# Pairwise products of 32 fields: eight-kilobyte packets for GpSimd's loads, and an output ring with three equal slots

## The chip, the cores and the metric

The kernel runs on one core of one Trainium2 chip. The metric is the time of one execution on the device, in microseconds (us), as the median of several runs. One execution was recorded by the hardware profiler; it has a time of its own beside the medians.

## The reference

There are 4096 rows of 32 fields with 64 numbers each, all in float32. For each of the 496 pairs of fields i < j, field i is multiplied with a 64 × 64 matrix of that pair, and the result is multiplied element by element with field j:

```
i_idx, j_idx = np.triu_indices(32, k=1)
vdotw = jnp.einsum('bpd,pde->bpe', inputs[:, i_idx, :], W)   # W: (496, 64, 64)
out = (vdotw * inputs[:, j_idx, :]).reshape(4096, 496 * 64)
```

The output has 4096 × 31,744 numbers, 520 MB. The inputs are 33.5 MB of rows and 8.1 MB of matrices.

## The kernel before, in words

**Tiles.** The rows are worked on in 32 tiles of 128 (NT in the code), one row on each of the 128 partitions. A tile has 31,744 output columns, 496 units of 64 columns. Of a tile's fields, two at a time make a pass: pass p has fields 2p and 2p+1, and its output is field 2p with all later fields, followed by field 2p+1 with all later ones. The loop (L198 to L248) runs over the tiles, in a tile over the passes, and in a pass over chunks of up to 512 columns.

**Compute.** TensorE transposes a tile's fields (L182), in two halves: the second at pass 3 of the tile itself, the first half of the next tile at pass 9. ACT copies them from PSUM to SBUF (L183). For each chunk TensorE multiplies the field 2p and the field 2p+1 with their weights (L222) into two banks of PSUM, taken round the eight banks. VectorE multiplies both with the later fields and writes the output ring in SBUF: one instruction with two rows of columns for a full chunk (L232), single ones for the ends (L240). The two rows that one instruction writes lie a whole field's width apart in the output, up to 31 units.

**The ring and the stores.** The ring (L185) has 28,160 columns, 440 units, for each partition. A tile is cut into four groups of passes (STORES, L17) with 118, 102, 123 and 153 units. Each group takes a place in the ring behind the one before; if it doesn't fit to the end, it begins at the ring's start (L204), and the rest of the ring stays unused that time. Behind a group SP issues one store of it (L246), 128 rows of 26 to 39 KB. VectorE must wait until the store that last read a place of the ring has landed.

**The loads.** There are three slots for tiles of x, filled two tiles at a time (x_slots, L34): tile 0 alone, tiles 1 and 2 at the start, then tiles 3 and 4 when tile 2 begins, and so on. The weights are resident; SP loads them in five pieces (L194) before the loop. Of a pair of tiles the odd one is loaded by ACT (L157), 8 KB for each partition. The even tiles 2 to 26 (LIGHT_TILES) are loaded by GpSimd, in another way (load_beside, L131); pairs without such a tile are loaded by ACT in one transfer, 16 KB for each partition.

**load_beside.** The 16 DMA engines share a transfer. The code holds[...] that engine 4 (LIGHT) should be given less to do. A tile is therefore loaded in two parts: 120 partitions (HEAD) by the fifteen engines other than LIGHT, and the last 8 partitions by two engines, other ones from tile to tile (PAIRS_FROM). [...] The fifteen engines take the 120 rows in two halves each, in packets of 4 KB. The host lays x out in the order in which it is read, with small gaps (PAD).

**Order.** SP's queue has the weights and then the stores in order of their groups. ACT's has its loads and the copies of the transposes, GpSimd's only its loads. Nothing else sets the order; each engine runs its program and waits on semaphores.

Of the kernel before, what the change touches and what calls it, by code (L numbers as in the profile page):

```python
# [9 lines left out]
F32 = mybir.dt.float32  # L10
ALU = mybir.AluOpType

P = 128
BANK = 512
BANKS = 8

STORES = [[0, 1], [2, 3], [4, 5, 6], [7, 8, 9, 10, 11, 12, 13, 14, 15]]  # L17

LOADS = [[0], [1], [2, 3], [4, 5, 6], [7, 8, 9, 10, 11, 12, 13, 14, 15]]


FIRST_HALF_AT, SECOND_HALF_AT = 9, 3
RING = 28160

DMA_ENGINES = 16
LIGHT = 4
LIGHT_TILES = range(2, 28, 2)
PAIRS_FROM = [6, 8, 10, 12, 14, 0, 1]
HEAD = P - P % (DMA_ENGINES - 1)
REST = (P - HEAD) // 2  # L30
PAD = 16


def x_slots(NT):  # L34


    loads = [[(0, 0)]]
    for t in range(1, NT, 2):
        if t + 1 == NT:
            loads.append([(t, 1)])  # L40
        elif loads[-1][-1] == (t - 1, 2):
            loads.append([(t + 1, 0), (t, 1)])
        else:
            loads.append([(t, 1), (t + 1, 2)])
    return loads


@with_exitstack
def pair_bilinear_kernel(
    ctx: ExitStack,  # L50
    tc: tile.TileContext,
    x: bass.AP,
    w: bass.AP,
    out: bass.AP,
    F: int,
    D: int,
):

    nc = tc.nc
    NT = out.shape[1] * 2 // (F * (F - 1) * D)
    NPR = F // 2

    width = [(F - 1 - i) * D for i in range(F)]
    off = [sum(width[:i]) for i in range(F)]
    cols = sum(width)


    woff = [i % 2 * D + sum(width[i % 2 : i : 2]) for i in range(F)]
    store_w = [sum(width[2 * p] + width[2 * p + 1] for p in g) for g in STORES]

    const = ctx.enter_context(tc.tile_pool(name="const", bufs=1))
    psum = ctx.enter_context(tc.tile_pool(name="ps", bufs=1, space=bass.MemoryType.PSUM))

    ident = const.tile([P, P], F32, tag="ident", name="ident")
    make_identity(nc, ident)

    def runs(tl, a, b, n):  # L100

        ap = tl[:, a : a + n]
        return bass.AP(ap.tensor, ap.offset, [list(ap.ap[0]), [b - a, 2], list(ap.ap[1])])

    xbuf = const.tile([P, 3 * F * D], F32, tag="x", name="x")
    x_loads = x_slots(NT)
    x_sizes = [
        sum(P * F * D + (2 * PAD if t in LIGHT_TILES else 0) for t, s in load) for load in x_loads
    ]
    slot = {t: xbuf[:, ts(s, F * D)] for load in x_loads for t, s in load}  # L110

    nudges = [const.tile([DMA_ENGINES, 16], F32, tag=f"nudge{i}", name=f"nudge{i}") for i in range(2)]
    cursor = 0

    def from_pool(out, in_):

        tc.keep_in_program_order(nc.gpsimd.dma_start(out=out, in_=in_))  # L117

    def from_engine(e):

        nonlocal cursor
        k = (e - cursor) % DMA_ENGINES
        if k:
            nudge = nudges[e == LIGHT + 1]
            from_pool(
                nudge[:k].rearrange("p (h c) -> p h c", h=2)[:, :, :4],
                x[: k * 8].rearrange("(p h c) -> p h c", p=k, h=2),
            )
        cursor = e

    def load_beside(at, xt, lap):  # L131

        nonlocal cursor
        n = F * D
        from_engine(PAIRS_FROM[lap % len(PAIRS_FROM)])
        g = REST * n + PAD
        tail = x[at + HEAD * n : at + HEAD * n + 2 * g].rearrange("(g c) -> g c", g=2)
        from_pool(xt[HEAD:], tail[:, : REST * n])
        cursor += 2
        from_engine(LIGHT + 1)  # L140
        from_pool(
            xt[:HEAD].rearrange("p (h c) -> p h c", h=2),
            x[at : at + HEAD * n].rearrange("(h p c) -> p h c", h=2, p=HEAD),
        )
        cursor = LIGHT

    def load_x(load):

        at = sum(x_sizes[: x_loads.index(load)])
        parts = [[(t, s)] for t, s in load] if any(t in LIGHT_TILES for t, s in load) else [load]  # L150
        for part in parts:
            t, s = part[0]
            n = len(part) * F * D
            if t in LIGHT_TILES:
                load_beside(at, slot[t], LIGHT_TILES.index(t))
            else:
                nc.scalar.dma_start(  # L157
                    out=xbuf[:, s * F * D : s * F * D + n],
                    in_=x[at : at + P * n].rearrange("(p c) -> p c", p=P),
                )  # L160
            at += P * n + (2 * PAD if t in LIGHT_TILES else 0)

    pring = psum.tile([P, BANKS * BANK], F32, tag="pring", name="pring")
    bank = 0

    def take_banks(n):

        nonlocal bank
        if bank + n > BANKS:
            bank = 0  # L170
        got = pring[:, bank * BANK : (bank + n) * BANK]
        bank = (bank + n) % BANKS
        return got

    xT = const.tile([P, NPR * P], F32, tag="xT", name="xT")

    def transpose_x(xt, g):

        n = 2 * BANK // P
        pt = take_banks(2)  # L180
        for c in range(n):
            nc.tensor.transpose(pt[:, ts(c, P)], xt[:, ts(n * g + c, P)], ident)  # L182
        nc.scalar.copy(xT[:, ts(g, 2 * BANK)], pt)  # L183

    ring = const.tile([P, RING], F32, tag="ring", name="ring")  # L185
    at = 0

    load_x(x_loads[0])
    w_sb = const.tile([P, sum(width[0::2])], F32, tag="w", name="w")
    done = 0  # L190
    for g in LOADS:

        upto = woff[2 * g[-1]] + width[2 * g[-1]]
        nc.sync.dma_start(out=w_sb[:, done:upto], in_=w[:, done:upto])  # L194
        done = upto

    transpose_x(slot[0], 0)
    for t in range(NT):  # L198
        xt = slot[t]
        for load in x_loads:  # L200
            if min(load)[0] == t + 1:
                load_x(load)
        for s, group in enumerate(STORES):
            if at + store_w[s] > RING:  # L204
                at = 0
            osb = ring[:, at : at + store_w[s]]
            at += store_w[s]
            o0 = off[2 * group[0]]
            for p in group:
                if p == SECOND_HALF_AT:  # L210
                    transpose_x(xt, 1)
                if p == FIRST_HALF_AT and t + 1 < NT:
                    transpose_x(slot[t + 1], 0)
                first = (width[2 * p] - 1) % BANK + 1
                for c1 in range(first, width[2 * p] + 1, BANK):
                    n = first if c1 == first else BANK
                    c0 = c1 - n
                    odd = width[2 * p + 1] and c1 > D
                    pm = take_banks(2)
                    for h in range(1 + bool(odd)):  # L220
                        a = woff[2 * p + h] + c0 - h * D
                        nc.tensor.matmul(  # L222
                            pm[:, h * BANK : h * BANK + n],
                            xT[h * D : (h + 1) * D, ts(p, P)],
                            w_sb[h * D : (h + 1) * D, a : a + n],
                            start=True,
                            stop=True,
                        )
                    xj = xt[:, (2 * p + 1) * D + c0 : (2 * p + 1) * D + c1]
                    o = [off[2 * p + h] - o0 + c0 - h * D for h in range(2)]  # L230
                    if odd and (c0 or c1 < width[2 * p]):
                        nc.vector.tensor_tensor(  # L232
                            runs(osb, o[0], o[1], n),
                            runs(pm, 0, BANK, n),
                            bass.AP(xj.tensor, xj.offset, [xj.ap[0], [0, 2], xj.ap[1]]),
                            ALU.mult,
                        )
                    else:
                        for h in range(1 + bool(odd)):
                            nc.vector.tensor_tensor(  # L240
                                osb[:, o[h] + h * D : o[h] + n],
                                pm[:, h * (BANK + D) : h * BANK + n],
                                xj[:, h * D :],
                                ALU.mult,
                            )
            nc.sync.dma_start(  # L246
                out=out[:, t * cols + o0 : t * cols + o0 + store_w[s]], in_=osb
            )  # L248


# [44 lines left out]
```

## Time and profile before

| | |
|---|---|
| median of 9 runs | 1325.56 us (1325.04 to 1326.89) |
| the profiled execution: its time | 1325.36 us |
| its span on the core | 1323.2 us |
| PE (TensorE) busy | 1165.3 us, 88% |
| DVE (VectorE) busy | 1183.5 us, 89% |
| ACT, POOL (GpSimd) busy | 66.1 us, 32.5 us |
| DMA: bytes, mean rate | 562.90 MB, 425 GB/s |
| the same stores, by group: issue to landing, median | 19.5, 17.6, 18.4 and 17.1 us (118, 102, 123 and 153 units) |
| ACT's loads of one tile, issue to landing | 18.9 us |
| GpSimd's loads of 120 partitions, issue to landing | 33.7 us |

The span is the time from the first to the last event on the core. An engine's busy time is the sum of its instructions' durations, where instructions that overlap count double. The DMA rows of the profile are those of the sixteen DMA engines together; "share" is the time that packets took, over sixteen times the span. A packet here is one contiguous piece that a DMA engine moves: for a store, one partition's row of the group. In the wait list, "A <- B: 75.2, 40, 6.1" means that engine A waited for B 75.2 us in total, 40 times, 6.1 us at the longest.

### The profile page before, as it was taken

What the parts mean: (1) busy time and instruction counts of PE and PEld (TensorE: products, weight loads), DVE (VectorE), ACT (ScalarE), POOL (GpSimd) and SP (SyncE); (2) the same over time, 40 slices, a digit from 0 to 9 for tenths busy, and PEclk for the clock granted to TensorE, in tenths of its full rate; (3) what the DMA queues carried; (4) which work ended last, traced back from release to release, by engine and by line L of the source; (5) the groups of instructions that cost most, each with busy time, mean ns of one, the idle gap of its engine ahead of it and who ended that gap; (6) DMA issues with size and microseconds to landing.
All of it is one profiled execution on the core that took longest, in us unless ns stands there. A gap on an engine that the chain in (4) does not pass through costs nothing.

```text
span 1323.2 us, 13175 instructions
## 1 busy us (share of the span) xinstructions
PE 1165.3 (88%) x5376; PEld 549.1 (41%) x5376; DVE 1183.5 (89%) x1376; ACT 66.1 (5%) x65; POOL 32.5 (2%) x58
## 2 busy tenths in 40 slices
PE   5998989989898998998989989898988989989893
PEld 3443444444343434444334444334444434443441
DVE  4998989989899998998989899898988989989894
ACT  0000000000000000000000000000000000000000
POOL 1000000000000000000000000000000000000000
PEclk9998999989999998998999999999999999999997
DMA  9999999999999999999999999999999999999998
GB/s 334 429 431 431 430 432 431 432 430 423 429 433 427 433 427 429 429 428 433 428 428 429 432 429 427 429 429 433 431 429 429 430 430 431 425 436 432 425 424 357
DMA packets 27068, 562.90 MB, mean 425 GB/s; under 512 B 4584, under 2 KB 4584, under 8 KB 7960
## 3 DMA queue, kind: packets, MB, share of 16 engines
q1 hardware_dynamic: 19152, 528.49, 93.4%
q10 hardware_dynamic: 2448, 19.92, 3.6%
q0 software_dynamic: 5408, 13.65, 2.7%
q8 instruction: 42, 0.69, 0.2%
q14 instruction: 18, 0.15, 0.0%
HBM read 41.95 MB, written 520.09 MB: 425 GB/s over the span
## 4 chain that ended last, share of the span: by engine, by line
DMA 47%; DVE 37%; issue 9%; PE 5%; DVEq 0%; ACT 0%
DMA out_dram<-ring 46%; DVE ring L232 32%; PE pring L222 5%; DVE ring L240 5%; DMA x<-in_x_dram 1%; PE pring L182 0%; DVEq L232 0%; ACT xT L183 0%; DVEq L291 0%; DVEq L240 0%
## 5 line engine op out<-in xcount | busy, mean ns | idle before, releaser
L222 PE MATMUL pring<-w,xT 64*128 64x512 f32 (+4 forms) x4864 | 1100.7, 563 | 128.6 <-DVE ring L232 111.3
L232 DVE TENSOR_TENSOR ring<-pring,x 128x1024 f32<-128x1024 f32 (+3 forms) x1056 | 1104.1, 1105 | 114.5 <-DMA out_dram<-ring 75.2
L222 PEld LDWEIGHTS pring<-w,xT 64*128 64x128 f32 x4864 | 491.8, 191 | 693.5 <-DVE ring L232 521.1
L183 ACT COPY xT<-pring 128x1024 f32<-128x1024 f32 x64 | 64.8, 1012 | 1212.1 <-PE pring L182 1189.7
L240 DVE TENSOR_TENSOR ring<-pring,x 128x64 f32<-128x64 f32 (+3 forms) x320 | 97.2, 352 | 7.4 <-DMA out_dram<-ring 6.5
L182 PEld LDWEIGHTS pring<-ident,x 128*128 128x128 f32 x512 | 57.2, 145 | 60.9 <-DVE ring L232 50.4
L182 PE MATMUL pring<-ident,x 128*128 128x128 f32 x512 | 72.5, 286 | 9.7 <-DMA x<-in_x_dram 9.7
L117 POOL DMA_DIRECT2D x<-in_x_dram x26 | 17.3, 665 | 910.2 <-DVE ring L240 910.2
L117 POOL DMA_DIRECT2D nudge<-in_x_dram x26 | 14.8, 568 | 4.3 <-DMA nudge<-in_x_dram 4.0
L183 ACT ACT_TABLE_LOAD x1 | 1.3, 1283 | 1.7 <-PEq L287 1.7
masks.py:199 POOL TENSOR_SCALAR_AFFINE_SELECT ident<-ident 128x128 f32<-128x128 f32 x1 | 0.3, 288 | 0.1
masks.py:197 POOL MEMSET ident<- 128x128 f32 x1 | 0.2, 205 | 0.3 <-POOLq L287 0.3
L287 POOL MEMSET const-float32-0.0<- 128x1 f32 x1 | 0.1, 93 | 0.2 <-issue 0.2
L287 POOL MEMSET const-bfloat16-1.0<- 128x1 bf16 x1 | 0.1, 96 | 0.0
L287 POOL MEMSET const-uint8-127<- 128x1 uint8 x1 | 0.1, 96 | 0.0
L287 POOL MEMSET const-float32-1.0<- 128x1 f32 x1 | 0.1, 93 | 0.0
## 6 DMA issues: line engine op xcount, KB each, us to landing
out_dram<-ring SPq DMA_DIRECT2D x32, 4896.0 KB, 17.1
out_dram<-ring SPq DMA_DIRECT2D x32, 3936.0 KB, 17.6
out_dram<-ring SPq DMA_DIRECT2D x32, 3776.0 KB, 18.4
out_dram<-ring SPq DMA_DIRECT2D x32, 3264.0 KB, 19.5
x<-in_x_dram ACTq DMA_DIRECT2D x15, 1024.0 KB, 18.9
x<-in_x_dram POOLq DMA_DIRECT2D x13, 960.0 KB, 33.7
x<-in_x_dram ACTq DMA_DIRECT2D x2, 2048.0 KB, 21.4
w<-in_w_dram SPq DMA_DIRECT2D x1, 2592.0 KB, 33.8
```

Of the source, the lines that this page charges most:

```text
L117: tc.keep_in_program_order(nc.gpsimd.dma_start(out=out, in_=in_))
L182: nc.tensor.transpose(pt[:, ts(c, P)], xt[:, ts(n * g + c, P)], ident)
L183: nc.scalar.copy(xT[:, ts(g, 2 * BANK)], pt)
L222: nc.tensor.matmul(pm[:, h * BANK : h * BANK + n], xT[h * D : (h + 1) * D, ts(p, P)], w_sb[h * D : (h + 1) * D, a : a + n], start=True, st ...
L232: nc.vector.tensor_tensor(runs(osb, o[0], o[1], n), runs(pm, 0, BANK, n), bass.AP(xj.tensor, xj.offset, [xj.ap[0], [0, 2], xj.ap[1]]), ALU ...
L240: nc.vector.tensor_tensor(osb[:, o[h] + h * D : o[h] + n], pm[:, h * (BANK + D) : h * BANK + n], xj[:, h * D :], ALU.mult,)
L287: nc = bacc.Bacc("TRN2", target_bir_lowering=False, num_devices=1)
```

## The change

**Loads.** LIGHT_TILES becomes 4, 6, 8, 10, 12, 14, 18, 20, 22, 24, 26, 28 and 30: thirteen tiles, as before. Tile 2 comes with tile 1 in one transfer of ACT's, and so does tile 16 with 15; the pairs 27 with 28 and 29 with 30, which did so before, now have a GpSimd tile each. In load_beside the fifteen engines get eight whole partitions each, one contiguous block of 64 KB in memory, in packets of 8 KB; a gap follows each block. The part for two engines is read first, as before.

**Ring and stores.** The ring has 440 units as before, and is now seen as a circle that the output runs round without regard to tiles. It is cut into three slots of 147, 147 and 146 units, one store for each; in the first round there are four stores, of 118, 102, 110 and 110 units. There are 110 stores instead of 128, and the last one has 32 units. A store is issued when all of its columns have been written, which `made` counts. Where an instruction's columns meet the ring's end, `multiply` cuts them in two; where its second row lies behind the end and its first ahead of it, there is one instruction for each row.

```diff
-STORES = [[0, 1], [2, 3], [4, 5, 6], [7, 8, 9, 10, 11, 12, 13, 14, 15]]
+ROUND = [147, 147, 146]
+FIRST_ROUND = [118, 102, 110, 110]
...
-RING = 28160
+RING_UNITS = sum(ROUND)
...
-LIGHT_TILES = range(2, 28, 2)
+LIGHT_TILES = [4, 6, 8, 10, 12, 14, 18, 20, 22, 24, 26, 28, 30]
 PAIRS_FROM = [6, 8, 10, 12, 14, 0, 1]
-HEAD = P - P % (DMA_ENGINES - 1)
-REST = (P - HEAD) // 2
+HEAD = P // DMA_ENGINES
+REST = HEAD // 2
 PAD = 16
...
+    ring_w = RING_UNITS * D
+    ends = [0]
+    while ends[-1] < NT * cols:
+        for units in ROUND if ends[-1] else FIRST_ROUND:
+            ends.append(min(ends[-1] + units * D, NT * cols))
+            if ends[-1] == NT * cols:
+                break
+    missing = [b - a for a, b in zip(ends, ends[1:])]
+    stored = 0
...
     def load_beside(at, xt, lap):
 
         nonlocal cursor
-        n = F * D
-        from_engine(PAIRS_FROM[lap % len(PAIRS_FROM)])
-        g = REST * n + PAD
-        tail = x[at + HEAD * n : at + HEAD * n + 2 * g].rearrange("(g c) -> g c", g=2)
-        from_pool(xt[HEAD:], tail[:, : REST * n])
-        cursor += 2
-        from_engine(LIGHT + 1)
-        from_pool(
-            xt[:HEAD].rearrange("p (h c) -> p h c", h=2),
-            x[at : at + HEAD * n].rearrange("(h p c) -> p h c", h=2, p=HEAD),
-        )
-        cursor = LIGHT
+        most = DMA_ENGINES - 1
+        for e, k, rows, p in (
+            (PAIRS_FROM[lap % len(PAIRS_FROM)], 2, REST, most * HEAD),
+            (LIGHT + 1, most, HEAD, 0),
+        ):
+            from_engine(e)
+            n = rows * F * D
+            blocks = x[at : at + k * (n + PAD)].rearrange("(k c) -> k c", k=k)
+            from_pool(xt[p : p + k * rows], blocks[:, :n])
+            at += k * (n + PAD)
+            cursor = (e + k) % DMA_ENGINES
...
-    ring = const.tile([P, RING], F32, tag="ring", name="ring")
-    at = 0
+    ring = const.tile([P, ring_w], F32, tag="ring", name="ring")
+
+    def multiply(tos, pm, xj, n):
+
+        at = [to % ring_w for to in tos]
+        cuts = {ring_w - a for a in at if a < ring_w < a + n}
+        for i, j in zip([0, *sorted(cuts)], [*sorted(cuts), n]):
+            a = [(to + i) % ring_w for to in tos]
+            if len(tos) == 2 and a[0] < a[1]:
+                xs = xj[:, i:j]
+                nc.vector.tensor_tensor(
+                    runs(ring, a[0], a[1], j - i),
+                    runs(pm, i, BANK + i, j - i),
+                    bass.AP(xs.tensor, xs.offset, [xs.ap[0], [0, 2], xs.ap[1]]),
+                    ALU.mult,
+                )
+                continue
+            for h, b in enumerate(a):
+                nc.vector.tensor_tensor(
+                    ring[:, b : b + j - i],
+                    pm[:, h * BANK + i : h * BANK + j],
+                    xj[:, i:j],
+                    ALU.mult,
+                )
+
+    def made(a, b):
+
+        nonlocal stored
+        for i in range(stored, len(missing)):
+            missing[i] -= max(0, min(b, ends[i + 1]) - max(a, ends[i]))
+        while stored < len(missing) and not missing[stored]:
+            a, b = ends[stored : stored + 2]
+            nc.sync.dma_start(
+                out=out[:, a:b], in_=ring[:, a % ring_w : a % ring_w + b - a]
+            )
+            stored += 1
...
-        for s, group in enumerate(STORES):
-            if at + store_w[s] > RING:
-                at = 0
...
+        for p in range(NPR):
...
+                o = [t * cols + off[2 * p + h] + c0 - h * D for h in range(2)]
+                if odd and (c0 or c1 < width[2 * p]):
+                    multiply(o, pm, xj, n)
+                else:
                     for h in range(1 + bool(odd)):
...
+                        multiply([o[h] + h * D], pm[:, h * (BANK + D) :], xj[:, h * D :], n - h * D)
+                for h in range(1 + bool(odd)):
+                    a = o[h] + (0 if c0 else h * D)
+                    made(a, o[h] + n)
```

The lines left out keep the transposes and the matrix multiplies as they are, and lay x out on the host to match.

## The prediction

> **What bounds the kernel now.** I read the page's slices of the span first, then the DMA queues, the waits of VectorE, and the windows of the start and the end. Slices and queues:
>
> ```profile
> DMA  9999999999999999999999999999999999999998
> GB/s 334 429 431 431 430 432 431 432 430 423 429 433 427 433 427 429 429 428 433 428 428 429 432 429 427 429 429 433 431 429 429 430 430 431 425 436 432 425 424 357
> ...
> q1 hardware_dynamic: 19152, 528.49, 93.4%
> q10 hardware_dynamic: 2448, 19.92, 3.6%
> q0 software_dynamic: 5408, 13.65, 2.7%
> q8 instruction: 42, 0.69, 0.2%
> ```
>
> The DMA engines are full in every slice but the first and the last, at about 430 GB/s, and the queues' shares add up to 99.9% of 16 engines' span. q1 is SP (stores and weights), q10 ACT's loads, q0 GpSimd's. The compute side is not the bound:
>
> ```profile
> DVE ring L232 <- DMA out_dram<-ring: 75.2, 40, 6.1
> ...
> DVE ring L240 <- DMA out_dram<-ring: 6.5, 6, 1.3
> ```
>
> VectorE waits 75.2 + 6.5 = 81.7 us for stores to free the ring. From 57.8 to 95.9 us (the second tile, with 0.7 us of such waits) its four stores are issued in 38.1 us, where the whole run needs 1323.2 / 32 = 41.3 us a tile. So the time is that of the DMA engines, and only work or idle time taken off them counts. Both lie at the edges, which the windows show (stretch, length, busy time of each engine, clock, DMA share, GB/s):
>
> ```profile
> core 0: us, PE busy (x) PEld busy (x) DVE busy (x) ACT busy (x) POOL busy (x), PEclk, DMA share, GB/s
> 2.00:8.00 6.00, 0.00 (x0) 0.00 (x0) 0.00 (x0) 0.94 (x1) 2.13 (x4) 1.00 0.93 369
> 8.00:14.00 6.00, 3.16 (x12) 2.38 (x14) 0.00 (x0) 1.01 (x1) 0.60 (x1) 1.00 1.01 322
> 14.00:22.00 8.00, 8.00 (x30) 3.21 (x28) 6.21 (x6) 0.00 (x0) 0.00 (x0) 1.00 1.07 312
> 22.00:26.00 4.00, 1.26 (x8) 1.15 (x8) 2.72 (x4) 0.00 (x0) 0.00 (x0) 0.86 1.01 318
> 26.00:34.00 8.00, 8.00 (x38) 5.14 (x36) 6.07 (x7) 1.01 (x1) 0.00 (x0) 0.85 1.01 430
> ...
> 60.00:1300.00 1240.00, 1116.93 (x5166) 523.89 (x5163) 1138.49 (x1321) 61.74 (x61) 26.72 (x44) 0.97 1.00 430
> ...
> 1310.00:1318.00 8.00, 0.00 (x0) 0.00 (x0) 0.00 (x0) 0.00 (x0) 0.00 (x0) 0.50 0.93 401
> 1318.00:1324.00 6.00, 0.00 (x0) 0.00 (x0) 0.00 (x0) 0.00 (x0) 0.00 (x0) 0.50 0.03 13
> ```
>
> Two things are to be seen. From 8 to 26 us the engines are busy but move only some 316 GB/s, against 430 right after. And from 1318 on nearly all of them are done while the span runs on. The trace's records of single packets (start, queue, bytes, duration; not the engine) say more of the end. Of the last store's 16 shares, 14 end from 1317.86 to 1318.35 us, one at 1319.03 and one at 1321.70; the span ends 1.5 us after that. The 14 had run dry before: the last store was issued at 1305.44, its first packet started at 1306.3, and eight packets of 1.448 us make 1317.9. So one slow engine, 3.7 us behind, sets the end. It shows elsewhere too: from 1200 us on about one store packet in sixteen takes some 2.6% longer (31,488 bytes: 1196 ns against 1166). After 1174 us, when no GpSimd loads are left, the last share of each store comes 0.20 to 0.32 us later than eight ordinary packets would, 1.05 us a tile of four stores.
>
> [...] 4,096 bytes take 159 ns, 8,192 take 309, 26,112 take 968, 39,168 take 1448, so a packet costs about 8.5 ns and its bytes at 27.2 per ns; the next packet starts 3 to 4 ns before the end of the one before, so 5 ns count.
>
> **Part 1: fewer, larger packets.** All bytes stay: 520.09 MB written, 41.95 MB read. Stores go from 128 to 110 (four, then 35 rounds of three, then one of 32 units of 64 columns). Per engine each has 8 packets and a semaphore write of 9 ns: 18 × 8 = 144 packets × 5 ns = 0.7 us, and 18 × 9 ns = 0.2 us. GpSimd's 13 tiles in 8 KB: 16 × (159 − 3.5) against 8 × (309 − 3.5) ns on 15 engines, 44 ns a tile, 0.6 us. Sum 1.5 us, on engines that are never free, so it comes off the end. With mean instead of usual durations, and nothing for the overlap, it is 1.3 + 0.2 + 0.9 = 2.4; the lower bound is 0.7, the store packets alone. I take 1.4.
>
> **Part 2: the start.** Tile 2 comes in ACT's 2 MB load, its packets 16 KB, not from GpSimd in 4 KB ones. Between 8 and 26 us 18 us × 316 GB/s = 5.7 MB moved; at 430 this takes 13.2 us, so 4.8 us were lost. With GpSimd's packets and weights alone (14 to 26 us) a 4 KB packet took about 213 ns instead of 159 and a 13,312-byte weight packet 735 where the fit above gives 498; when GpSimd's ended, at 26 us, weights ran at full speed. But from 8 to 14 us, where ACT's tile 1 still ran and GpSimd had moved little, packets were slow too (7,424 bytes: about 375 ns instead of 281), while weights beside tile 0 had been at full speed until 8 us. So GpSimd's small reads may be the cause, or any second stream. Bounds: all 4.8 us won, or 1 us lost if ACT's larger packets hold the second weight piece back until TensorE, which now waits 2.7 us for the third piece, waits for the second as well. I take 2.4, half of the loss. Cover: the last weight packet then ends near 33.6 us instead of 36.0, and stores must be there. Tile 0 now issues at 24.6, 35.6, 44.6 and 57.8; the previous store still had 9.3, 8.1 and 4.2 us to go at the last three. In the changed one the first store is the same 118 units, the third and fourth are shorter (110 against 123 and 153) and the ring isn't reused before 440 units, so some 3 us of cover should remain; beyond that a faster start buys idle engines.
>
> **Part 3: the end, and the slow engine.** A GpSimd tile spares one engine its sixteen packets, 16 × 155.5 ns = 2.5 us, and puts a mean of 0.2 us on the others. Two tiles cost the slow engine 2 × 1.05 = 2.1 us, so it gains 0.6 us per pair while such loads run. Before, the last one (tile 26) is issued in tile 24, near 1010 us; from there 310 us × 1.05 / 41.3 = 7.9 us are lost, and what lead it had was capped by the ring, hence 3.7 behind. After, the loads go to tile 30, issued in tile 28 near 1165 us, and only 3.8 us are lost. Followed from the start: −2.3 + 2.7 = +0.4 at tile 4, +3.3 at tile 14, −4.2 + 2.7 for the gap at 16, +5.2 at tile 30, −4.2 to the end: about +1, so it is no longer last. And the end isn't dry: the last store has 32 units (eight 8 KB packets, 2.5 us), and when the ring lets VectorE begin it, two slots of some 11 us each are still with the engines. What is late next: the mean over the engines and the one with 32 KB more tails (1.2 us, the 1319.03 above). Mean end before: (14 × 1318.0 + 1319.0 + 1321.7) / 16 = 1318.3, and idle time ahead of the last stores makes it about 1317.5; plus 1.2 is 1318.7, so 3.0 us are won. Bounds: 1.0 (the lead is capped again) and 4.2 (perfectly even).
>
> **Part 4: the ring.** Working through the code's loop, operations that meet the ring's end are cut, or their two rows taken apart: 1483 VectorE instructions instead of 1376. The seven small ones of a tile take 2.40 us for 1792 columns, so about 0.09 us each beyond the columns: 107 × 0.09 = 9.6 us over the run, hidden by VectorE's 81.7 us of waiting. Without that cover it would be 9.6 us. Queued behind a waiting VectorE operation are all later ones, then TensorE (two banks each) and SP's next store. Two rows of a pair lie up to 31 units apart, so VectorE meets the next slot's wait with the present one unfinished; by the code's order up to 4.2 us of work is then left. Steady state: the slot two back lands, 4.2 us of VectorE, 0.33 us of issue and 0.9 us to the first packet, while the engines hold a full slot, 147 units × 64 × 4 bytes × 128 at 430 GB/s = 11.2 us. Over 5 us remain, no less than the 3.8 us seen before, so I take 0. Bounds: a gain of 0.5 us (short idle times of fast engines gone), a loss of 0.1 us a store. SP waits for VectorE as now and issues 18 times less; POOL's and ACT's waits for a tile's end stay, ACT's 17 loads and GpSimd's 26[...] keep their number.
>
> **Sum.** 1.4 + 2.4 + 3.0 + 0 = 6.8 us off the profiled execution, 1325.36 (its span 1323.2 and 2.2 around it): 1318.6. It lies 0.2 under the median 1325.56, so 1318.8.
>
> **Rivals.** (a) All of it pays: GpSimd's small reads cause the whole slow start and the end is even: 2.0 + 4.8 + 4.2 = 11.0, 1314.6. For it: weights alone run at full speed. Against: the slow packets at 8 us, and the thin cover. (b) Only the packets and part of the end: ACT's 2 MB beside the weights is as slow: 1.4 + 1.5 = 2.9, 1322.7. For it: any two streams may collide. (c) Slower: the three slots let the engines run dry. VectorE stops at a slot's border with rows unfinished, the store is issued late, and some engine is idle ahead of its first packet. It decides from 6.8 / 107 = 0.06 us of idle time a store; at 0.13 us it costs 13.9, net +7.1, 1332.7. Against it: the 5 us of reserve. That the change doesn't do what it says (the slow engine not spared) would cost up to 13 × 2.5 = 32 us; the old 8 KB tails show that the form works.
>
> **Chances.** Forecast 0.45 (1316.8 to 1321), (a) 0.17, (b) 0.28, half of it within 0.2% (over 1322.9; 0.2% or 2.65 us is about what a measurement can tell from no change), (c) with the failure of the relief 0.10. So faster 0.45 + 0.17 + 0.14 = 0.76, same 0.14, slower 0.10. The range takes most of (a) and two thirds of (b): 1314.0 to 1324.0.
>
> **What would show it.** Right: 8,192-byte packets of about 309 ns on q0; weights landing 2 us earlier, over 316 GB/s between 8 and 26 us; the last store's shares ending within 1.5 us of each other near 1313; VectorE still waiting 60 us or more for stores. Wrong: DMA shares under 0.98 in the middle, a store's first packet 1 us after its issue in most slots, or a last engine over 2 us behind.

## The result and the profile after

The changed kernel takes 1319.58 us (median of 10 runs, 1317.34 to 1322.88), the one before 1325.98 us (31 runs, 1325.04 to 1327.79). The ratio is 0.9953, with a 95% interval from 0.9945 to 0.9961: 0.5% faster, 6.4 us. The forecast was 1318.8. The profiled execution took 1321.35 us (span 1319.6), 1.8 us above the median, so the profile accounts for 4.0 of the 6.4 us.

The slices and DMA queues of the changed kernel:

```profile
DMA  9999999999999999999999999999999999999998
GB/s 393 433 429 431 431 433 429 432 430 430 432 427 427 431 431 428 434 429 435 429 430 428 426 432 429 429 429 431 423 430 428 427 427 424 414 437 430 429 431 354
...
q1 hardware_dynamic: 16560, 528.49, 93.3%
q10 hardware_dynamic: 2448, 19.92, 3.7%
q0 software_dynamic: 3744, 13.65, 2.6%
```

The bytes are the same, q1 has 2592 packets less and q0 1664 less. The first slice went from 334 to 393 GB/s. But the slice from 1122 to 1155 us has 414, less than any inner slice had before (423).

VectorE's waits for the ring, and then the windows:

```profile
DVE ring L203 <- DMA out_dram<-ring: 49.7, 32, 4.8
...
DVE ring L211 <- DMA out_dram<-ring: 19.4, 17, 2.7
```

```profile
core 0: us, PE busy (x) PEld busy (x) DVE busy (x) ACT busy (x) POOL busy (x), PEclk, DMA share, GB/s
...
8.00:14.00 6.00, 4.37 (x14) 2.75 (x16) 0.52 (x1) 1.01 (x1) 0.00 (x0) 1.00 0.99 421
14.00:22.00 8.00, 7.70 (x38) 3.43 (x36) 7.40 (x8) 0.00 (x0) 0.00 (x0) 1.00 1.01 432
22.00:26.00 4.00, 3.79 (x20) 1.76 (x19) 4.00 (x5) 0.97 (x1) 0.00 (x0) 1.00 1.06 457
26.00:34.00 8.00, 8.00 (x40) 3.22 (x36) 8.00 (x9) 0.04 (x1) 0.00 (x0) 1.00 1.02 406
...
60.00:1300.00 1240.00, 1131.92 (x5156) 532.11 (x5156) 1144.77 (x1429) 61.74 (x61) 26.53 (x47) 0.97 1.00 429
...
1306.00:1310.00 4.00, 0.00 (x0) 0.00 (x0) 0.00 (x0) 0.00 (x0) 0.00 (x0) 0.50 0.97 420
1310.00:1316.00 6.00, 0.00 (x0) 0.00 (x0) 0.00 (x0) 0.00 (x0) 0.00 (x0) 0.50 0.59 252
1316.00:1320.00 4.00, 0.00 (x0) 0.00 (x0) 0.00 (x0) 0.00 (x0) 0.00 (x0) 0.50 0.06 25
```

VectorE still waits 69.1 us in total, and the DMA share is 1.00 from 60 to 1300 us, so the DMA engines are still the bound. The start runs at full rate (421 to 457 GB/s from 8 to 26 us, where it was 312 to 322), and the last weight packet ends at 30.5 us instead of 36.0. A packet counts wholly in the window in which it starts, so a short window can show a rate above the steady 430, or a share above 1.00 (457 GB/s and 1.06 from 22 to 26 us). The end is not the even one that was forecast: in the windows the DMA share falls off slowly, from 0.97 over 0.59 to 0.06. By the packet records the sixteen engines end between 1312.9 and 1318.05 us.

### The profile page after: what moved, and what is told of

It is laid out like the page before. It is cut to its first block, busy times and chain, and to the rows that moved or that the text cites. A ratio compares the mean times of both kernels' runs of the same rounds, so it can differ in the third digit from the quotient of the medians.

```text
span 1319.6 us, 13188 instructions
## 1 busy us (share of the span) xinstructions
PE 1180.3 (89%) x5376; PEld 554.7 (42%) x5376; DVE 1190.5 (90%) x1483; ACT 66.1 (5%) x65; POOL 30.2 (2%) x58
## 4 chain that ended last, share of the span: by engine, by line
DMA 54%; DVE 32%; issue 6%; PE 6%; DVEq 0%; ACT 0%
DMA out_dram<-ring 54%; DVE ring L203 27%; PE pring L258 6%; DVE ring L211 5%; DMA x<-in_x_dram 1%; PE pring L190 0%; DVEq L203 0%; ACT xT L191 0%; DVEq L319 0%; DVEq L211 0%
## 5 line engine op out<-in xcount | busy, mean ns | idle before, releaser
L258 PE MATMUL pring<-w,xT 64*128 64x512 f32 (+4 forms) x4864 | 1117.2, 562 | 101.6 <-DVE ring L203 82.6
L203 DVE TENSOR_TENSOR ring<-pring,x 128x1024 f32<-128x1024 f32 (+4 forms) x1012 | 1043.5, 1089 | 87.2 <-DMA out_dram<-ring 49.7
L258 PEld LDWEIGHTS pring<-w,xT 64*128 64x128 f32 x4864 | 499.2, 191 | 677.9 <-DVE ring L203 477.6
L211 DVE TENSOR_TENSOR ring<-pring,x 128x64 f32<-128x64 f32 (+7 forms) x471 | 169.0, 410 | 20.4 <-DMA out_dram<-ring 19.4
```

Of the source, the lines that this page charges most:

```text
L203: nc.vector.tensor_tensor(runs(ring, a[0], a[1], j - i), runs(pm, i, BANK + i, j - i), bass.AP(xs.tensor, xs.offset, [xs.ap[0], [0, 2], xs ...
L211: nc.vector.tensor_tensor(ring[:, b : b + j - i], pm[:, h * BANK + i : h * BANK + j], xj[:, i:j], ALU.mult,)
L258: nc.tensor.matmul(pm[:, h * BANK : h * BANK + n], xT[h * D : (h + 1) * D, ts(p, P)], w_sb[h * D : (h + 1) * D, a : a + n], start=True, st ...
```

## The experiments

Each engine's work can be taken from the packet records. I use the prediction's fit to the records of before, 8.5 ns + bytes / 27.2 (159 ns for 4,096 bytes, 1448 for 39,168), as a packet's clean duration, and call what lies above it its excess, summed over the packets and divided by 16. The slow engine can be followed as a chain of packets, each some 1 to 4% too long, each starting where the one before ends. Its lag is the mean start of its packets, less that of all packets of the same store, here for the stores from 1200 to 1280 us; below zero it is ahead, and an empty place means that it was not followed. "While later loads run" takes the packets that start after 36 us and between the first and the last packet of a load; how closely neighbouring loads are joined moves such a sum by some 0.5 us. The table is from the profiled executions, one of each kernel, in us; the times are medians of all runs. The e, f and g kernels ran on three different chips, each group beside the kernel before, which took 1326.16, 1326.27 and 1326.31 us there.

| kernel | time | excess to 36 us | excess while later loads run | mean end | last end | slow engine's lag |
|---|---|---|---|---|---|---|
| before | 1325.98 | 5.9 | 3.6 | 1318.3 | 1321.7 | +3.0 |
| changed | 1319.58 | 1.3 | 6.6 | 1314.8 | 1318.1 | +0.4 |
| e1_ring_only | 1322.25 | 5.9 | 3.6 | 1316.1 | 1318.7 | +1.5 |
| e2_loads_only | 1322.39 | 1.6 | 4.6 | 1315.4 | 1318.2 | +0.9 |
| e3_start_only | 1319.43 | 1.6 | 3.3 | 1313.1 | 1315.6 | +1.4 |
| e4_pool_at_start | 1323.14 | 6.3 | 4.5 | 1317.0 | 1319.2 | |
| f1_ring_4k_to28 | 1317.19 | 1.4 | 3.8 | 1311.9 | 1313.5 | +0.5 |
| f2_8k_to28 | 1318.53 | 1.4 | 5.1 | 1313.0 | 1315.2 | +0.2 |
| f3_8k_wide_gap | 1320.06 | 1.3 | 6.1 | 1314.5 | 1317.5 | |
| f4_ring_4k_newlist | 1317.88 | 1.4 | 4.1 | 1312.1 | 1314.6 | +0.4 |
| g1_pool_plain_at_start | 1317.83 | 1.3 | 4.2 | 1312.2 | 1314.7 | −0.1 |
| g2_8k_plain_rows | 1341.65 | 1.5 | 16.4 | 1332.3 | 1338.4 | +6.7 |
| g3_2k_packets | 1320.46 | 1.3 | 5.3 | 1313.5 | 1316.3 | +1.4 |
| g4_fourteen_tiles | 1319.49 | 1.4 | 5.6 | 1314.1 | 1317.5 | −0.7 |

**The parts alone.** e1_ring_only is the changed kernel with load_beside, the host's layout and the tiles of before. e2_loads_only is the kernel before with those three of the changed one. e3_start_only changes one line of the kernel before:

```diff
-LIGHT_TILES = range(2, 28, 2)
+LIGHT_TILES = range(4, 30, 2)
```

> The new ring and its 110 stores, with the loads of the kernel before (GpSimd's 4 KB packets, tiles 2 to 26). Theory A (the start belongs to the loads, the end mostly to the choice of tiles): the slow start between 8 and 26 us is still there (near 316 GB/s), only the store packets (0.9 us) and a part of the dry end (about 1 us) come off: ratio to before near 0.9985, 1324 us. Rival B (the ring does most of it): 1320 to 1321 us, ratio near 0.996.

> The loads of the changed kernel (8 KB packets, tiles 4 to 30 without 16, tile 2 from ACT) with the ring and the 128 stores of before. Theory A: the start runs at full rate (over 420 GB/s from 8 to 26 us, 4.4 us won), 0.6 to 0.9 us for the packets, and the slow engine is not behind at the end (2 us): 1318.5, ratio near 0.9945. Rival B (the ring does most of it): 1322 to 1324, ratio near 0.998.

> The kernel before with one number changed: GpSimd's thirteen tiles are 4 to 28 instead of 2 to 26, so tile 2 comes with tile 1 from ACT, and the last tile for GpSimd is one later; packets stay at 4 KB, the ring is the old one. If GpSimd's stream is what makes the start slow: 8 to 26 us over 420 GB/s and 4.4 us won, and the slow engine ends up to 2 us less behind: 1319.5 to 1321.5, ratio near 0.996. If any second stream beside the weights is slow: the start stays near 320 GB/s and the time is 1324 to 1326.

Ratios to the kernel before, with intervals: 0.9970 (0.9958 to 0.9981), 0.9970 (0.9960 to 0.9980) and 0.9949 (0.9937 to 0.9961). The start of e3_start_only:

```profile
8.00:14.00 6.00, 4.34 (x14) 2.74 (x16) 0.49 (x1) 1.01 (x1) 0.00 (x0) 1.00 1.02 435
14.00:22.00 8.00, 7.83 (x38) 3.50 (x36) 7.38 (x8) 0.00 (x0) 0.00 (x0) 1.00 1.00 426
22.00:26.00 4.00, 3.79 (x20) 1.81 (x20) 4.00 (x5) 0.93 (x1) 0.00 (x0) 1.00 1.04 448
```

One line wins as much as the whole change, 6.7 us. Of the 6.1 us by which its last engine ends earlier, 4.3 are excess that the start no longer has; the line also gives GpSimd a later last tile, and the slow engine's lag falls from 3.0 to 1.4. The start is at full rate as soon as GpSimd's tile 2 is gone from it, with the 4 KB packets and the old ring still there; in e1_ring_only it is as slow as before. Theory A held for the start. It failed for the rest: the ring wins 3.9 us alone instead of 2 (the slow engine's lag falls from 3.0 to 1.5 with the same tiles; that the new ring lets it keep more of its lead is a guess), and e2_loads_only, which has the fast start too, is 3.0 us slower than e3_start_only. The two differ in the packets' form and in the list of tiles. So something in the new loads costs time.

**The start again.** e4_pool_at_start is the changed kernel with tile 2 put in front of its list of tiles.

> The changed kernel with tile 2 given back to GpSimd, in 8 KB packets (fourteen tiles for GpSimd). If GpSimd's stream at the start is the cause whatever its packets: the start falls to some 320 GB/s again and the time rises by 4 us over the changed kernel, to 1323.5. If the 4 KB packets were the cause: a start at 400 GB/s or more and within 1 us of the changed kernel. The fourteenth tile spares the slow engine 2.5 us more and gives the others 0.2 us each, which moves the time by less than 1 us either way.

Its ratio is 0.9979 (0.9969 to 0.9988), its median 3.6 us over the changed kernel's, and its start is slow again with packets of 8 KB:

```profile
8.00:14.00 6.00, 3.24 (x12) 2.41 (x14) 0.00 (x0) 1.01 (x1) 0.51 (x1) 1.00 1.04 306
14.00:22.00 8.00, 6.74 (x28) 3.03 (x26) 6.22 (x6) 0.00 (x0) 0.00 (x0) 1.00 1.03 255
22.00:26.00 4.00, 0.86 (x5) 0.03 (x1) 2.67 (x3) 0.00 (x0) 0.00 (x0) 1.00 0.99 390
```

So the small size of the packets is not the cause. Is it GpSimd's stream, as a third one beside two others? g1_pool_plain_at_start starts from f1_ring_4k_to28 (below) and loads tile 2 by GpSimd in the plain form, a row of 8 KB for each of 128 partitions in one transfer, with no small load of its own:

```diff
-                nc.scalar.dma_start(
+                start = from_pool if t == 2 else nc.scalar.dma_start
+                start(
```

The host lays tile 2 out by itself, and ACT loads tile 1 alone.

> The new ring, 4 KB form, tiles 4 to 28 (as f1_ring_4k_to28, which had ratio 0.9935), but tile 2 is loaded by GpSimd at the start in the plain form, 128 rows of 8 KB over all sixteen engines[...]. If any third stream at the start makes reads slow: some 310 GB/s from 8 to 26 us again, start excess near 5.5 us instead of 1.35, 1321.5, ratio near 0.9965. If it was the form for fifteen engines: start at full rate, ratio near 0.9935.

```profile
8.00:14.00 6.00, 3.12 (x12) 2.34 (x14) 0.00 (x0) 1.01 (x1) 0.00 (x0) 1.00 1.02 430
14.00:22.00 8.00, 7.81 (x36) 3.53 (x36) 6.65 (x7) 0.00 (x0) 0.00 (x0) 1.00 1.01 431
22.00:26.00 4.00, 4.00 (x20) 1.58 (x20) 4.00 (x5) 0.00 (x0) 0.00 (x0) 1.00 1.06 456
```

Ratio 0.9935 (0.9923 to 0.9947). By the packet records GpSimd's load runs from 5.5 to 12.9 us, beside ACT's tile 1 and the weights, and the packets of all three take their clean durations; the excess to 36 us is 1.3 us, as in the changed kernel. So neither the number of streams nor GpSimd's queue makes the start slow, but the form of load_beside: a tile in two parts (in the records of before never more than two of the small part's eight packets run at once), and the small loads of from_engine (0.1 to 0.4 KB) ahead of them.

No run separates these, but the records say when it begins. In the kernel before, the first 4 KB packet of the fifteen-engine part starts at 11.1 us. From 8 to 11 us GpSimd has moved only the two-engine part (eight packets, 6.9 to 10.0 us) and small loads, and already ACT's packets take 1.3 to 1.7 times their clean duration and the weights' 1.2 to 1.6 times. So the fifteen-engine part can't be the cause alone. One small load of from_engine isn't it either: in g1_pool_plain_at_start one runs between 12 and 15 us, and the packets beside it are not slowed.

**The cost in the new loads.** f1_ring_4k_to28 is e1_ring_only with e3_start_only's line. f2_8k_to28 is the changed kernel with that line. f4_ring_4k_newlist is the changed kernel with the old load_beside. f3_8k_wide_gap is the changed kernel with another gap:

```diff
-PAD = 16
+PAD = 128
```

> The new ring with GpSimd's old 4 KB form and its thirteen tiles 4 to 28: the two parts that won most alone, together. Theory C (the 8 KB form costs some 3 us and hides what the ring wins): the ring's part comes on top of the start's: 1315.5 to 1317, ratio 0.992 to 0.9935. Theory D (ring and tile list repair the same uneven end, so they don't add): 1318.5 to 1319.5, ratio near 0.995.

> The changed kernel with one number changed: GpSimd's tiles are 4 to 28 without a gap, still in 8 KB packets. Theory C (the form is what costs): as the changed kernel, 1319 to 1321, and as widely spread from run to run (3 us or more). If the list with its gap at 16 costs: 1316 to 1317.5, and 1 us of spread.

> The changed kernel with gaps of 512 bytes instead of 64 behind each 64 KB block, so that every block begins at a multiple of 512 bytes. If the 8 KB form costs because its blocks, and the tiles behind them, lie across such borders: 1316 to 1317 and a small spread. If it costs for another reason (the packet's size, or fifteen contiguous streams): no change, 1319 to 1321.

> The changed kernel with the old 4 KB form alone: new ring, tiles 4 to 30 without 16. Theory C (the form costs 3 us): 1316 to 1317, a small spread, average work of an engine 1.3 us less than in the changed kernel. If the list costs: 1319 to 1320, as the changed kernel. The forecast's own term for the packets: 0.6 us slower than the changed kernel.

| | 8 KB form | 4 KB form |
|---|---|---|
| tiles 4 to 30 without 16 | changed: 1319.58 (0.9945 to 0.9961) | f4: 1317.88 (0.9925 to 0.9948) |
| tiles 4 to 28 | f2: 1318.53 (0.9935 to 0.9959) | f1: 1317.19 (0.9923 to 0.9947) |

In both rows the 8 KB form has the longer median, by 1.7 and 1.3 us; half of theory C's 3 us, and against the forecast's own term, which had it 0.6 us faster. The intervals of the ratios overlap, so each pair alone doesn't settle it. f3_8k_wide_gap, which has the 8 KB form and the list with the gap at 16, ran in the same group as f4_ring_4k_newlist and took 1320.06 us (0.9942 to 0.9968), 2.2 us more. The packet records point the same way: while loads run, the excess is 5.1 and 6.6 us in the two kernels of this table with 8 KB and 3.8 and 4.1 in the two with 4 KB. In f2_8k_to28 and f1_ring_4k_to28 it sits mostly on the stores beside the loads (4.3 against 3.2 us). So a cost of the form is likely, and of 1 to 2 us. The list of tiles makes 0.7 and 1.1 us, too little to tell. f3_8k_wide_gap is not faster than the changed kernel either; nothing speaks for the blocks' alignment as the cause.

Theory D failed too: f1_ring_4k_to28 is 2.2 us faster than e3_start_only, which differs only in the ring (four of its five runs lie under all five of e3_start_only; the intervals of the ratios overlap). f1_ring_4k_to28 has the shortest median of the study. Its end, to be set against that of the changed kernel:

```profile
1300.00:1306.00 6.00, 0.00 (x0) 0.00 (x0) 0.00 (x0) 0.00 (x0) 0.00 (x0) 0.50 0.92 400
1306.00:1310.00 4.00, 0.00 (x0) 0.00 (x0) 0.00 (x0) 0.00 (x0) 0.00 (x0) 0.50 0.94 405
1310.00:1316.00 6.00, 0.00 (x0) 0.00 (x0) 0.00 (x0) 0.00 (x0) 0.00 (x0) 0.50 0.21 90
```

The share from 1310 us on is 0.21 where the changed kernel has 0.59 and then 0.06: the engines end between 1310.3 and 1313.5 us.

**Packet size and relief.** Two kernels change f1_ring_4k_to28 in the number of pieces that a row of the fifteen engines is read in, on the host and here:

```diff
-            xt[:HEAD].rearrange("p (h c) -> p h c", h=2),
-            x[at : at + HEAD * n].rearrange("(h p c) -> p h c", h=2, p=HEAD),
+            xt[:HEAD].rearrange("p (h c) -> p h c", h=1),
+            x[at : at + HEAD * n].rearrange("(h p c) -> p h c", h=1, p=HEAD),
```

> As f1_ring_4k_to28, with the 120 rows in one piece of 8 KB each instead of two halves of 4 KB; no gaps between the fifteen engines' shares. If the packet's size makes the stores beside it slow: store packets beside loads lose 1 us more than with 4 KB, and the time is 1318 to 1319 (ratio 0.994 to 0.995), as in f2_8k_to28. If the gapped blocks do it: as f1_ring_4k_to28 less 0.5 us for the packets, 1316.7 (ratio 0.993).

> As f1_ring_4k_to28, with packets of 2 KB for GpSimd's 120 rows (four quarters). The packets' own cost: 16 more per engine and tile, 13 x 16 x 5 ns = 1.0 us more. If smaller packets leave the stores alone more: the stores' loss beside loads falls by some 0.5 us or more, so 1317.2 to 1317.8 (ratio 0.9935 to 0.994). If size has nothing to do with it: 1318.2 (ratio 0.9943).

Neither could answer its question. g2_8k_plain_rows (h = 1) has 8 KB packets but a ratio of 1.0116 (1.0103 to 1.0129), 24.5 us more than f1_ring_4k_to28. Its slow engine lies 6.7 us behind, where in the others that were followed it is between 0.7 ahead and 3.0 behind. That is what the forecast's failure case looked like, the slow engine not spared, priced at up to 32 us. The trace doesn't name engines, but it shows what follows a slow store packet (1.5 to 5% too long) while GpSimd loads, wherever just one packet starts as it ends: in this kernel one of GpSimd's load packets in 77 of 98 cases, in f1_ring_4k_to28 in 22 of 82, where ordinary store packets have one behind them in 2286 of 2449. So in the form with h = 1 the slow engine does get load packets. The 16.4 us of excess while loads run, 8.0 of it on GpSimd's own packets, come almost all from the fifth load on, near 380 us; why is open, and how the 24.5 us divide between the two is not shown. g3_2k_packets (h = 4) still has 3120 packets of 4,096 bytes on q0 in the records, so a packet here seems to hold two pieces. It has a ratio of 0.9965 (0.9953 to 0.9977), slower than 4 KB pieces by 3.3 us, with more excess while loads run (5.3 against 3.8 us). Neither larger nor smaller pieces than 4 KB were better.

g4_fourteen_tiles is f1_ring_4k_to28 with `range(4, 32, 2)`.

> As f1_ring_4k_to28, with a fourteenth tile (30) from GpSimd, so the slow engine is spared 2.5 us more near the end; in f1_ring_4k_to28 it was 1.2 us behind the mean there and the last to end, 1.6 us after the mean. Expected: it is ahead of the mean at the end, the others have 0.2 us more, another engine is last by 1 to 2 us: 1316.3 to 1317.5, ratio 0.993 to 0.9938. If the slow engine's lag sets the end alone: 1.2 us less than f1_ring_4k_to28, 1316.0.

1319.49 us, ratio 0.9949 (0.9937 to 0.9961): not the expected gain. The slow engine is ahead (a lag of −0.7 us), as expected, but the last engine ends 3.4 us after the mean, and the excess while loads run is 5.6 us. Sparing the slow engine further didn't pay: the median is 2.3 us over that of f1_ring_4k_to28.

## Why the prediction was right, point by point

The median was right to 0.8 us, the composition was not: errors of both signs cancelled, so that close a meeting is luck. The profiled execution of the changed kernel is one of its slower ones: it missed the forecast for it, 1318.6, by 2.8 us. By the packet records of the two profiled executions the mean end moved from 1318.3 to 1314.8, and these terms add up to 3.7 us, where 6.8 were forecast:

| term, us | forecast | measured |
|---|---|---|
| the start | −2.4 | −4.7 (excess to 36 us, 5.9 to 1.3) |
| the packets' own cost | −1.4 | −1.2 (clean durations 1305.3 to 1303.3, less 3.5 ns of overlap a packet) |
| slower packets while loads run | 0 | +3.0 (3.6 to 6.6) |
| the rest of the mean end | about −0.8 of idle time at the end | −0.6, as what is left over |
| last engine behind the mean | from 3.4 to 1.2 | from 3.4 to 3.2 |

Of the +3.0, by queue, 1.2 lie on the stores, 1.0 on ACT's loads and 0.8 on GpSimd's own packets. Part of it may belong to this slow execution rather than to the kernel.

**What bounds the kernel: right.** VectorE's waits stay at 69.1 us, over the 60 that were named.

**Part 1, packets: right in the count, wrong in what stands beside it.** 144 store packets of each engine and half of GpSimd's fell away for 1.2 us. Step that failed: "44 ns a tile, 0.6 us" took a load packet as costing only its own clean time. With the 8 KB form packets are slower while loads run (5.1 us of excess against 3.8, f2_8k_to28 against f1_ring_4k_to28), and instead of a 0.6 us gain the medians show a loss of 1.3 to 2.2, in pairs whose intervals overlap.

**Part 2, the start: right mechanism, undersized.** It was taken at half, 2.4 us, for want of a reason to choose. The trace before showed slow packets also from 8 to 14 us, with little moved by GpSimd, and I read that as a hint at any second stream; load_beside's two-engine part was already at work then. The whole 4.7 us belonged to load_beside; the upper bound, 4.8, was nearly met. The cover held: the stores' reserve (the last end of the store before, less the next one's issue) was never under 5.9 us in the changed kernel.

**Part 3, the end: half right.** The slow engine's lag fell from 3.0 to 0.4 us, which is the right direction but less than the count, which had it ahead at that time and still about 1 us ahead at the end (its sum takes 3.8 us in one place and 4.2 in another for the same last stretch). The last engine was as far behind the mean as before, 3.2 us; with a lag of 0.4 us the slow one is hardly it, so another one now. Step that failed: "the mean over the engines and the one with 32 KB more tails (1.2 us)". It took the other fifteen as even, but their ends lie apart: 5.1 us from the first end to the last, where 1.5 were named. That the excess beside the loads falls unevenly on them is a likely cause, not a shown one: with 3.8 us of it f1_ring_4k_to28 has its last engine 1.6 us behind the mean, near the forecast, but f4_ring_4k_newlist and g1_pool_plain_at_start, with 4.1 and 4.2 us, have 2.5.

**Part 4, the ring: right that it costs nothing.** 107 more VectorE instructions stayed hidden. From e3_start_only to f1_ring_4k_to28 the median falls by 2.2 us; in the profiles 1.2 of it are at the mean end, near the 0.9 of Part 1 for its packets, and 0.9 the last engine being closer to the mean.

**Rivals.** (c), engines run dry, did not happen: the share is 1.00 from 60 to 1300 us. (a) was right on the start and wrong on the even end. (b) was right that part of the end would not come. The spread of the runs, 5.5 us where the kernel before has 2.8, was not foreseen. The other kernels spread from 0.7 (g2) and 0.9 us (e3, g1) to 6.1 (f3), and the excess in their profiles doesn't order them. Only profiled runs have packet records, so the cause of the spread stays open.

**Open.** What in load_beside's form slows the packets beside it, and why one tile costs 4.7 us at the start where twelve among stores have 3.6 us of excess in all; and why pieces of 8 KB and of 2 KB are worse there than 4 KB (by 1.3 to 1.7 us and by 3.3 us in the medians). No run tells these apart.

## What to carry to other kernels

Where the DMA engines are the bound (here a share of 1.00 from 60 to 1300 us), count what a load does to the packets beside it besides its own packets, and read it from the packets' durations. It can be the larger part: in the kernel before, tile 2 had (240 × 159 + 8 × 309 ns) / 16 = 2.5 us of packets of its own, as a mean over the engines, and its form brought 4.7 us of excess at the start. Among stores the same form was cheap: while all later loads ran, twelve of its tiles among them, the excess was 3.6 us. So look at the start apart from the steady stretch, and keep such a form out of it where it costs. Try the one-line part of a change alone: here it won as much as the whole, and with the new ring and without the new packets the median was 8.8 us under that of the kernel before, 1317.19 us.

## What was not expected of the hardware

Up to about one store packet in sixteen (3 to 6% of them in each stretch from 60 to 1300 us, in both profiles) takes 1 to 4% longer, on one engine as far as the chain can be followed, and this stops about when the compute engines have finished. In the kernel before, the chain of long packets ends at 1307.8 us (VectorE's last instruction ends near 1305.4), and that engine's last store runs at 1448 ns a packet like all others; in the changed kernel the two times are 1299.9 and 1298.1 us. Two kernels agree on the coincidence; its cause is not shown. The same load of 1 MB beside weights and a second load cost nothing in the plain form (1.3 us of excess to 36 us in g1_pool_plain_at_start, where the changed kernel, with tile 2 from ACT, has 1.3) and some 4.7 us in load_beside's form (5.9 in the kernel before). And 120 rows read in one piece each took 24.5 us more over the run than the same rows read in two halves of 4 KB (1341.65 against 1317.19 us).
